# Column tiles for the 384-column products of the second pass, in a four-layer graph kernel

## The chip, the cores and the metric

The kernel runs on one core of one Trainium2 chip. The metric is the device time of one execution in microseconds (us); less is better. The core's engines each work through their own instruction stream in order: TensorE (PE, with its weight loads shown apart as PEld), VectorE (DVE), ScalarE (ACT), GpSimd (POOL) and SyncE (SP), which here issues most of the DMA transfers. Engines wait for each other by semaphores.

## The reference, cut to what matters

There are 32 graphs (batches) of 512 nodes with 128 features, each with a symmetric 0/1 adjacency matrix. Four layers follow one another, and each adds its result to `x`:

```python
h = relu(layernorm(x))                       # before each layer
# layer 0: masked attention
q, k, v = relu(h @ Wq.T + bq), relu(h @ Wk.T + bk), relu(h @ Wv.T + bv)
x = x + softmax(mask(q @ k.T, adj)) @ v
# layer 1: convolution of the last 128 nodes -> LSTM over 128 steps -> gates a normalized aggregation
dyn = conv(h[:, -128:, :]); lw = lstm(dyn)
x = x + sigmoid((A_norm @ h) @ lw)
# layer 2: four graph layers with skip connections; layer 3: one aggregation, a product and a PReLU
x = x + layer2(h, adj);  x = x + prelu(adj @ (h @ W.T) + bias)
```

What matters for the order of the work is layer 1. Its LSTM needs layer 0's result for the last 128 nodes of all 32 batches, and then runs 128 steps one after another. The layers from 1 on need its end.

## The kernel before

The kernel is one program of some 26,400 instructions. The function `symmetric` builds a list of operations, and a planner (`class Plan`) puts them in order with assumed durations. The order that it finds is each engine's fixed instruction stream; on the chip nothing is reordered by it any more.

**The stages.**

- *Pass 1* (`pass_1(b)`, ranks from 10,000): for each batch, `x` is loaded and normalized, keys and values are computed, layer 0 is finished for the last 128 nodes alone, and the convolution fills the LSTM's input `seq`. Keys, normalized input and values go to DRAM.
- *The LSTM* (`lstm()`, ranks 0 to 127, all below `URGENT`): 128 steps. A step's products have a 128-row by 32-column weight tile (the hidden state of 32 batches), so four of them, each for another 32 features, stand side by side in the array and run together. This is what the code calls tiled (`tiled=True`). Each step has 16 matrix instructions of this kind (`f_z`, L1212), since an fp32 product is two instructions.
- *Pass 2* (`pass_2(b)`, ranks from 20,000): layer 0 for the other 384 nodes of each batch. It is independent of the LSTM and is meant to fill the engines beside it. Per batch it has one query product `f_pq` (L1291) and four score products `f_s` (L1300), each 128 by 128 by 384 columns, then an exponential (L1303), a product with the mask (L1304), twelve products `f_po` (L1309) and an update of `x`. For batches in `EARLY` (0 to 19) layer 1's aggregation `f_pg` (L1395) is done here too.
- *The rest* (`rest(b, turn, lw_after)`, ranks from 30,000): layers 1 to 3 of each batch, after the LSTM.

**What sets the order.** An operation's rank is its priority. The planner takes for each engine the operation that can start earliest, and among those that can start at once the lowest rank. A rank of 30,000 or more is replaced by a due time. `LATE = 4` gives the pass 2 of the last four batches such a rank, so that they are due among the first turns of the rest; `FIRST` names the two batches before them, whose rest comes first. Two costs are written into the planner for a change between tiled and other products on TensorE, of which this is the first and this the place that makes it count in the choice:

```python
    SWITCH = (0.2, 0.1)          # to a product that is not tiled, to one that is
    ...
                    if e == "PE" and o.tiled != tiled and rank >= self.spared:
                        s = max(s, free[e] + self.SWITCH[o.tiled])
```

`self.spared` is 20,000. So after a tiled operation a tiled one that is ready starts 0.2 sooner than one that is not tiled, whatever the ranks; after one that is not tiled, it is the tiled one that comes 0.1 later. The LSTM's steps are kept from delay by `held`: an operation of rank 1000 or more is not started where it would run more than 0.15 us beyond the expected start of a step.

**Buffers.** `BUFS` gives the number of each tag; the tags `ar`, `x`, `inv`, `n0` to `n3` and `a` are handed out in the order in which the program names them. PSUM has eight banks (`mm`).

**Transfers and warming.** `DMA` books a transfer on SP and adds `gap=2.0` us until its data counts as landed. `warm_up` books products on a tile of zeros, whose results nobody reads, in front of the first real products: 16 at the start, and 16 more in the last turn.

Of the kernel before, what the change touches and what calls it, by code (L numbers as in the profile page):

```python
# [13 lines left out]
P = 128  # L14
# [6 lines left out]
W_Q, W_K, W_V, W_CONV, W_IH, W_HH = 0, 1, 2, 3, 6, 10  # L21
# [731 lines left out]
def symmetric(ctx, tc, x, adj, weights, cols, rows, lstm_b, prelu_a, out, fail):  # L753
# [12 lines left out]
    nc = tc.nc  # L766
# [3 lines left out]
    L = NT - 1  # L770
    NR = N - P
    MANY = 512 // (4 * B)
    LATE = 4
    FIRST = [B - LATE - 2 + k for k in range(2)]
    EARLY = range(20)
    FOLDS = (4, 7, 10, 13)
    MOVED = range(2, B - 2)
    TURN = 32
# [3 lines left out]
    BUFS = {"a": 2, "ar": 6, "x": 7, "xn": 5, "y": 5, "gs": 5, "inv": 4, "n0": 4, "n1": 4, "n2": 4, "n3": 4, "low": 3, "hp": 2, "dt": 2, "mm": 8, "st": 4, "mv": 4, "rs": 4, "sh": 4, "dg": 8, "dv": 4,  # L782
            "ri": 3, "th": 3, "c": 3, "cu": 2, "cv": 2, "tcn": 2, "h": 2}
# [10 lines left out]
    plan = Plan(BUFS, ("ar", "x", "inv", "n0", "n1", "n2", "n3", "a"), "mm")  # L794
# [4 lines left out]
    def f32(ap):  # L799
        return ap.bitcast(FP)  # L800
# [5 lines left out]
    def new(tag, shape, name, dtype=FP):  # L806
        return plan.cell(sb, tag, shape, dtype, name)

    def bank(name, shape=(P, 512), whole=True, filled=False):
        return plan.cell(ps, "mm", shape, FP, name, whole, filled)  # L810


    def t_mm(n):
        return max(0.222, n * 0.001676)
# [6 lines left out]
    def t_act(n):  # L821
        return 0.17 + n * 0.0006

    def t_dve(n):
        return 0.145 + n * 0.00088

    def t_dma(kb):
        return 0.1 + kb / 315.0

    def PE(rank, t, fn, r=(), w=(), **k):  # L830
        return plan.op({"PE": (t, fn)}, rank, r, w, **k)

    def ACT(rank, t, fn, r=(), w=(), **k):
        return plan.op({"ACT": (t, fn)}, rank, r, w, **k)

    def DVE(rank, t, fn, r=(), w=(), **k):
        return plan.op({"DVE": (t, fn)}, rank, r, w, **k)

    def POOL(rank, t, fn, r=(), w=(), **k):
        return plan.op({"POOL": (t, fn)}, rank, r, w, **k)  # L840

    def DMA(rank, kb, fn, r=(), w=(), **k):
        return plan.op({"SP": (max(0.45, t_dma(kb)), fn)}, rank, r, w, gap=2.0, **k)

    def turn_tiles(dst, src):

# [37 lines left out]
    w = const.tile([P, W_SD[0] + 1, P], FP, name="f_w")  # L884
# [27 lines left out]
    for j in range(P // TURN):  # L912
        part = bass.ts(j, TURN)
# [8 lines left out]
    def warm_up(rank, t, name, after=()):  # L922

        c = bank(name)
        PE(rank, t, lambda: nc.tensor.matmul(c.t, marks[:, :P], marks, start=True, stop=True), [], [c], after=after)

    for k in range(2 * BUFS["mm"]):
        warm_up(HEAD, 0.43 if k < 8 else 0.216, f"f_warm_{k}")

    def bias_row(rank, k, row, r):  # L930
# [174 lines left out]
    def pass_1(b):  # L1105
        R = 10_000 + b * 10
        xc = new("x", (P, NT, P), f"f_x_{b}")
        DMA(R, 256, lambda: nc.sync.dma_start(xc.t, x[b].rearrange("(t p) d -> p t d", p=P)), [], [xc])
        al = new("n1", (P, NT, P), f"f_al_{b}")
        DMA(R + 11, 256, lambda: nc.sync.dma_start(al.t, adj[b, :, NR:].rearrange("(t p) i -> p t i", p=P)), [], [al])  # L1110
        xn = ln_full(R, xc, f"a{b}")
# [36 lines left out]
        s = bank(f"f_sl_{b}", (P, NT, P))  # L1148
# [117 lines left out]
    def pass_2(b):  # L1266
        R = 20_000 + b * 10 if b < B - LATE else 30_000 + (b - B + LATE) * 10 + 15
        dkq, dv, dl, dx = kept[b]
        early = b in EARLY
        whole = early or b in FIRST  # L1270
        a = new("a" if whole else "ar", (P, NT, N if whole else NR), f"f_a_{b}")
        keys = new("inv", (P, N), f"f_k2_{b}")
        hT = new("xn", (P, NR), f"f_h2_{b}")
        v = new("n3", (P, NT, P + 1), f"f_v2_{b}")
        xc = new("x", (P, NT if whole else L, P), f"f_x2_{b}")
        DMA(R, 192, lambda: nc.sync.dma_start(hT.t, dkq.t[:, N:]), [dkq], [hT])
        DMA(R, 256, lambda: nc.sync.dma_start(keys.t, dkq.t[:, :N]), [dkq], [keys])
        if whole:
            DMA(R, 1024, lambda: nc.sync.dma_start(a.t, adj[b].rearrange("(t p) j -> p t j", p=P)), [], [a])
            ar, deg = squares(R, b, a, "2")  # L1280
            mask, rows_of = ar, lambda j: f32(ar.t[:, j, :NR])
        else:
            DMA(R, 768, lambda: nc.sync.dma_start(a.t, adj[b, :, :NR].rearrange("(t p) j -> p t j", p=P)), [], [a])
            mask, rows_of = a, lambda j: a.t[:, j, :]
        DMA(R, 258, lambda: nc.sync.dma_start(v.t, dv.t), [dv], [v])
        DMA(R, 192, lambda: nc.sync.dma_start(xc.t[:, :L, :], x[b, :NR].rearrange("(t p) d -> p t d", p=P)), [],
            [(xc, t) for t in range(L)])
        if whole:
            DMA(R, 64, lambda: nc.sync.dma_start(xc.t[:, L, :], dl.t), [dl], [(xc, L)])
        pq = bank(f"f_pq_{b}", (P, NR), whole=False)  # L1290
        PE(R, t_mm(NR), lambda: nc.tensor.matmul(pq.t, w[:, W_Q, :], hT.t, start=True, stop=True), [hT], [pq])  # L1291
        q = new("xn", (P, NR), f"f_q_{b}")
        plan.op({
            "ACT": (t_act(NR) + 0.09, lambda: nc.scalar.activation(q.t, pq.t, AF.Relu, bias=colb[:, C_Q : C_Q + 1])),
            "DVE": (t_dve(NR), lambda: nc.vector.tensor_scalar(q.t, pq.t, colb[:, C_Q : C_Q + 1], 0.0, OP.add, OP.max)),
        }, R, [pq], [q])
        es = []
        for j in range(NT):
            s = bank(f"f_s_{b}_{j}", (P, NR), whole=False)
            PE(R, t_mm(NR), lambda s=s, j=j: nc.tensor.matmul(s.t, keys.t[:, bass.ts(j, P)], q.t, start=True, stop=True),  # L1300
               [keys, q], [s])
            e = new(f"n{j}" if j < 3 else "y", (P, NR), f"f_e_{b}_{j}")
            ACT(R, t_act(NR), lambda s=s, e=e: nc.scalar.activation(e.t, s.t, AF.Exp), [s], [e])  # L1303
            DVE(R, t_dve(NR), lambda e=e, j=j: nc.vector.tensor_mul(e.t, e.t, rows_of(j)), [(mask, j)], [e])  # L1304
            es.append(e)
        po = bank(f"f_po_{b}", (P, L, P + 1), whole=False)
        for t in range(L):
            for j in range(NT):
                PE(R, t_mm(P), lambda t=t, j=j: nc.tensor.matmul(  # L1309
                    po.t[:, t, :], es[j].t[:, bass.ts(t, P)], v.t[:, j, :], start=(j == 0), stop=(j == NT - 1)),  # L1310
                    [es[j], v], [po])
        ri = plan.fixed(None)
        sum_ops.append(DVE(R, 0.21, lambda: nc.vector.reciprocal(rinv[:, b, :L], po.t[:, :, P]), [po], [ri]))
        for t in range(L):
            DVE(R, 0.26, lambda t=t: nc.vector.scalar_tensor_tensor(xc.t[:, t, :], po.t[:, t, :P], rinv[:, b, t : t + 1],
                                                                    xc.t[:, t, :], OP.mult, OP.add), [po, ri], [(xc, t)])
        if whole and not early:
            begun[b] = a, xc, ar, deg
        else:
            DMA(R + 5, 192, lambda: nc.sync.dma_start(dx.t, xc.t[:, :L, :]), [(xc, t) for t in range(L)], [dx])  # L1320
        mv = ln_stats(R, xc, range(L), f"r{b}")
        l1 = lns[b]
        POOL(R, 0.15, lambda: nc.gpsimd.tensor_copy(ln1[:, b, 0, :L], mv.t[:, :L, 0]), [mv], [(l1, "mr")])
        ln_rstd(R, mv, 0, L, (lambda: ln1[:, b, 1, :L], (l1, "rr")))
        if early:
            d = new("dg", (P, NT), f"f_d2_{b}")

            def root():
                nc.gpsimd.tensor_scalar_add(d.t, deg.t, 1.0)
                nc.gpsimd.tensor_tensor(d.t, d.t, neg_half[:, 0, :], OP.pow)  # L1330
            POOL(R, 1.3, root, [deg], [d])
            rs = new("rs", (P, NT), f"f_rs_2{b}")
            POOL(R, 0.34, lambda: nc.gpsimd.tensor_mul(rs.t, ln1[:, b, 1, :], d.t), [d, l1], [rs])
            gT, _ = sums_of_1(R, b, xc, ar, rs)
            dg = plan.fixed(dram.tile([P, N], FP, tag=f"g{b}", name=f"f_dgT_{b}"))
            DMA(R + 5, 256, lambda: nc.sync.dma_start(dg.t, flat(gT.t)), [gT], [dg])
            kept_sums[b] = dg
# [5 lines left out]
    def squares(rank, b, a, name):  # L1343

        ar = new("ar", (P, NT, N), f"f_ar{name}_{b}", FR)
        deg = new("dg", (P, NT), f"f_deg{name}_{b}")
        for t in range(NT):
            ACT(rank, 0.62, lambda t=t: nc.scalar.activation(ar.t[:, t, :], a.t[:, t, :], AF.Square,  # L1348
                                                             accum_out=deg.t[:, t : t + 1]), [a], [(ar, t), (deg, t)])
        return ar, deg  # L1350
# [226 lines left out]
    for b in range(B):  # L1577
        pass_1(b)
# [94 lines left out]
```

## Time and profile before

| | before |
|---|---|
| time, median of 3 runs | 1316.56 us (1314.63 to 1316.73) |
| span of the profiled run | 1316.2 us |
| busy: PE, PEld | 1288.5, 990.8 us |
| busy: DVE, ACT, POOL | 999.4, 826.0, 392.7 us |
| granted TensorE clock, mean | 0.995 |
| LSTM steps on TensorE | 188.4 to about 506 us |

A line of the profile's groups reads: line of the code, engine, operation, output tile and input tiles, shapes, count, then busy time and mean nanoseconds of one, then the idle time of the engine ahead of them and what ended it. Matrix products are pipelined: the duration of one includes its way through the array, so two that follow each other overlap, and the distance between their starts is what each costs. A line of the timeline reads: start, length, engine, line, operation, output and inputs, count merged into the line.

### The profile page before, as it was taken

What the parts mean: (1) busy time and instruction counts of PE and PEld (TensorE: products, weight loads), DVE (VectorE), ACT (ScalarE), POOL (GpSimd) and SP (SyncE); (2) the same over time, 40 slices, a digit from 0 to 9 for tenths busy, and PEclk for the clock granted to TensorE, in tenths of its full rate; (3) what the DMA queues carried; (4) which work ended last, traced back from release to release, by engine and by line L of the source; (5) the groups of instructions that cost most, each with busy time, mean ns of one, the idle gap of its engine ahead of it and who ended that gap; (6) DMA issues with size and microseconds to landing.
All of it is one profiled execution on the core that took longest, in us unless ns stands there. A gap on an engine that the chain in (4) does not pass through costs nothing. (4 is left out here: it accounts for less than half of the span.)

```text
span 1316.2 us, 26405 instructions
## 1 busy us (share of the span) xinstructions
PE 1288.5 (98%) x8829; PEld 990.8 (75%) x8829; DVE 999.4 (76%) x3392; ACT 826.0 (63%) x2084; POOL 392.7 (30%) x729
## 2 busy tenths in 40 slices
PE   8999999999999999999999999999999999999996
PEld 6888876776766766777777787787877877877774
DVE  7888878887788788766588668777777887787744
ACT  5666667777765655676387547576665675675433
POOL 4655533321221133331142224132232332332101
PEclk8999999999999999999999999999999999999999
DMA  7888888887676656975568766767645566673211
GB/s 230 266 262 271 261 282 288 265 278 238 204 245 199 194 176 108 229 191 139 105 135 218 166 153 128 193 151 152 156 120 120 121 136 140 142 168 64 54 28 36
DMA packets 298817, 230.69 MB, mean 175 GB/s; under 512 B 138032, under 2 KB 245808, under 8 KB 298672
## 3 DMA queue, kind: packets, MB, share of 16 engines
q1 hardware_dynamic: 281776, 212.13, 57.4%
q0 software_dynamic: 16896, 16.78, 8.3%
q8 instruction: 72, 1.18, 0.4%
q14 instruction: 73, 0.60, 0.2%
HBM read 135.80 MB, written 61.60 MB: 150 GB/s over the span
## 5 line engine op out<-in xcount | busy, mean ns | idle before, releaser
L1395 PE MATMUL f_pa<-f_ar,f_y 128*128 128x512 f32 x1024 | 292.8, 422 | 0.7 <-ACT f_y L1377 0.7
L1395 PEld LDWEIGHTS f_pa<-f_ar,f_y 128*128 128x128 f32 x1024 | 188.2, 188 | 66.2 <-issue 28.0
L1489 PE MATMUL f_py<-f_wf,f_n 128*128 128x128 f32 x1280 | 173.9, 275 | 0.2 <-ACT f_n L1504 0.2
L1489 PEld LDWEIGHTS f_py<-f_wf,f_n 128*128 128x128 f32 x1280 | 163.8, 192 | 9.2 <-ACT f_n L1504 1.9
L1504 ACT ACTIVATE f_n<-f_pa,f_bcol 128x512 f32<-128x512 f32 x128 | 88.0, 689 | 110.5 <-PE f_pa L1500 107.2
L1500 PE MATMUL f_pa<-f_n,f_wf 128*128 128x512 f32 x320 | 152.7, 593 | 1.1 <-DVE f_pa L1496 1.1
L1348 ACT ACTIVATE f_ar<-f_a 128x512 fp32r<-128x512 f32 x208 | 129.1, 622 | 13.4 <-DMA f_a<-in_adj_dram 6.7
L1377 ACT CAST f_y<-f_py 128x512 fp32r<-128x512 f32 x128 | 74.6, 583 | 87.0 <-PE f_py L1489 81.5
L1309 PEld LDWEIGHTS f_po<-f_v,f_e 128*128 128x128 f32 x768 | 100.7, 190 | 25.5 <-issue 10.9
L1496 DVE TENSOR_TENSOR f_pa<-f_pa,f_inv 128x512 f32<-128x512 f32 x128 | 87.5, 693 | 41.0 <-PE f_pa L1395 40.5
L1378 DVE TENSOR_TENSOR f_y<-f_py,f_y 128x512 fp32r<-128x512 f32 x128 | 87.3, 684 | 34.5 <-ACT f_y L1377 34.4
L1309 PE MATMUL f_po<-f_v,f_e 128*128 128x129 f32 x768 | 112.7, 282 | 0.6 <-DVE f_e L1304 0.6
L1300 PE MATMUL f_s<-f_q,f_k 128*128 128x384 f32 x256 | 99.7, 500 | 0.0
L1457 POOL DMA_DIRECT2D f_das<-f_ar x32 | 28.8, 899 | 230.9 <-ACT f_ar L1348 126.4
L1500 PEld LDWEIGHTS f_pa<-f_n,f_wf 128*128 128x128 f32 x320 | 56.8, 190 | 44.5 <-issue 37.0
L1462 DVE SCALAR_TENSOR_TENSOR f_junk<-f_a,f_aT 128x1024 bf16<-128x1024 f32 x64 | 78.1, 1221 | 7.6 <-DMA f_aT<-f_das 6.5
L1212 PE MATMUL f_z<-f_w,f_seq 128*32 128x128 f32 x2040 | 82.2, 279 | 1.6 <-DVE f_seq L1260 0.6
L1395 PE MATMUL f_pg<-f_ar,f_xp_d 128*128 128x512 f32 x256 | 77.9, 428 | 0.0
L1212 PEld LDWEIGHTS f_z<-f_w,f_seq 128*32 128x32 f32 x2040 | 48.3, 109 | 37.4 <-ACT f_e L1303 7.2
L1395 PE MATMUL f_pg<-f_ar,f_xp_c 128*128 128x512 f32 x256 | 72.4, 412 | 0.3 <-ACT f_xp_c L1385 0.3
L1489 PE MATMUL f_py<-f_wf,f_T_c 128*128 128x128 f32 x448 | 72.7, 275 | 0.0
L1303 ACT ACTIVATE f_e<-f_s 128x384 f32<-128x384 f32 x128 | 61.2, 487 | 16.1 <-PE f_s L1300 14.5
(203 smaller groups left out, 2738.7 us busy)
## 6 DMA issues: line engine op xcount, KB each, us to landing
f_a<-in_adj_dram SPq DMA_DIRECT2D x52, 1024.0 KB
f_das<-f_ar POOLq DMA_DIRECT2D x32, 512.0 KB, 5.3
f_dkq<-f_kh SPq DMA_DIRECT2D x32, 448.0 KB
f_dv<-f_v SPq DMA_DIRECT2D x32, 258.0 KB
f_v<-f_dv SPq DMA_DIRECT2D x32, 258.0 KB
f_x<-in_x_dram SPq DMA_DIRECT2D x32, 256.0 KB
f_al<-in_adj_dram SPq DMA_DIRECT2D x32, 256.0 KB
f_k<-f_dkq SPq DMA_DIRECT2D x32, 256.0 KB
```

Of the source, the lines that this page charges most:

```text
L1212: nc.tensor.matmul(z.t[part, k, :, :], h, w[:, m : m + 4, part], start=False, stop=True, skip_group_check=True)
L1300: PE(R, t_mm(NR), lambda s=s, j=j: nc.tensor.matmul(s.t, keys.t[:, bass.ts(j, P)], q.t, start=True, stop=True), [keys, q], [s])
L1309: PE(R, t_mm(P), lambda t=t, j=j: nc.tensor.matmul(po.t[:, t, :], es[j].t[:, bass.ts(t, P)], v.t[:, j, :], start=(j == 0), stop=(j == NT - ...
L1348: ACT(rank, 0.62, lambda t=t: nc.scalar.activation(ar.t[:, t, :], a.t[:, t, :], AF.Square, accum_out=deg.t[:, t : t + 1]), [a], [(ar, t), ...
L1377: ACT(rank, t_act(N), lambda: nc.scalar.copy(parts.t[:, :, 0, :], src.t), [src], [(parts, 0)])
L1378: DVE(rank, t_dve(N), lambda: nc.vector.tensor_sub(parts.t[:, :, 1, :], src.t, f32(parts.t[:, :, 0, :])), [src, (parts, 0)], [(parts, 1)])
L1395: nc.tensor.matmul(pg.t, parts.t[:, j, k, :], ar.t[:, j, :], start=(k == 0 and j == 0), stop=(k == 1 and j == NT - 1))
L1462: nc.vector.scalar_tensor_tensor(junk, flat(a.t[:, 2 * k : 2 * k + 2, :]), 1.0, flat(aT.t[:, 2 * k : 2 * k + 2, :]), OP.mult, OP.not_equal ...
L1489: nc.tensor.matmul(py.t[:, j, :], nodes[n].t[:, bass.ts(j, P)], wf[:, W_F[i] + c, 0, :], start=False, stop=(c == nch - 1), skip_group_chec ...
L1496: before = DVE(R, t_dve(N), lambda pa=pa: nc.vector.tensor_mul(pa.t, pa.t, inv_row.t), [inv_row], [pa])
L1500: nc.tensor.matmul(pa.t, wf[:, W_F[i] + c, 1, :], nodes[n].t, start=False, stop=(c == nch - 1), skip_group_check=True)
L1504: ACT(R, 0.57, lambda pa=pa, n=n, i=i: nc.scalar.activation(n.t, pa.t, AF.Tanh, bias=bcol[:, i : i + 1]), [pa], [n])
```

## The change

Four edits are made.

- The query and score products of pass 2 are written as four products of 32 columns of the stationary matrix each, one per column tile of the array (`by_columns`), and are booked with `tiled=True`. The result in PSUM is the same. The aim is that they stand beside the LSTM's tiled products without a change of the array's mode.
- `LATE` becomes 5: the pass 2 of one more batch (27) is due among the first turns of the rest, and `FIRST` becomes batches 25 and 26.
- The planner's landing time of the loads of `x` in pass 1 is 2.0 us for batch 0, 4.5 us for batches 1 to 3 and 3.5 us for the others, where it was 2.0 us for all.
- The products that warm TensorE at the start become 20, where they were 16 (`2 * BUFS["mm"]`).

```diff
-    LATE = 4
+    LATE = 5
     FIRST = [B - LATE - 2 + k for k in range(2)]
...
     def DMA(rank, kb, fn, r=(), w=(), **k):
-        return plan.op({"SP": (max(0.45, t_dma(kb)), fn)}, rank, r, w, gap=2.0, **k)
+        return plan.op({"SP": (max(0.45, t_dma(kb)), fn)}, rank, r, w, gap=k.pop("gap", 2.0), **k)
+
+    def by_columns(out, left, right):
+        for c in range(P // TURN):
+            part = bass.ts(c, TURN)
+            nc.tensor.matmul(out[part], left[:, part], right, start=True, stop=True)
...
-    for k in range(2 * BUFS["mm"]):
+    for k in range(20):
         warm_up(HEAD, 0.43 if k < 8 else 0.216, f"f_warm_{k}")
...
-        DMA(R, 256, lambda: nc.sync.dma_start(xc.t, x[b].rearrange("(t p) d -> p t d", p=P)), [], [xc])
+        DMA(R, 256, lambda: nc.sync.dma_start(xc.t, x[b].rearrange("(t p) d -> p t d", p=P)), [], [xc],
+            gap=2.0 if b == 0 else 4.5 if b < 4 else 3.5)
...
-        PE(R, t_mm(NR), lambda: nc.tensor.matmul(pq.t, w[:, W_Q, :], hT.t, start=True, stop=True), [hT], [pq])
+        PE(R, t_mm(NR), lambda: by_columns(pq.t, w[:, W_Q, :], hT.t), [hT], [pq], tiled=True)
...
-            PE(R, t_mm(NR), lambda s=s, j=j: nc.tensor.matmul(s.t, keys.t[:, bass.ts(j, P)], q.t, start=True, stop=True),
-               [keys, q], [s])
+            PE(R, t_mm(NR), lambda s=s, j=j: by_columns(s.t, keys.t[:, bass.ts(j, P)], q.t),
+               [keys, q], [s], tiled=True)
```

## The prediction

> **What bounds the kernel now.** I read the page's first part, then the busy times by stage, then the timeline of TensorE inside the LSTM's stage, and last the head of the run. The page says that TensorE is the engine to look at.
>
> ```profile
> PE 1288.5 (98%) x8829; PEld 990.8 (75%) x8829; DVE 999.4 (76%) x3392; ACT 826.0 (63%) x2084; POOL 392.7 (30%) x729
> ```
>
> The stages, cut at the LSTM's first step, its last, and the last product of pass 2:
>
> ```profile
> core 0: us, PE busy (x) PEld busy (x) DVE busy (x) ACT busy (x) POOL busy (x), PEclk, DMA share, GB/s
> 0.00:188.00 188.00, 179.83 (x1278) 152.95 (x1279) 154.59 (x687) 115.63 (x227) 96.57 (x247) 0.98 0.83 262
> 188.00:507.00 319.00, 315.68 (x3260) 219.94 (x3259) 257.85 (x1179) 223.18 (x781) 80.77 (x152) 1.00 0.72 226
> 507.00:545.00 38.00, 35.06 (x223) 28.86 (x222) 30.70 (x107) 22.64 (x59) 14.32 (x25) 1.00 0.89 183
> 545.00:1316.00 771.00, 757.94 (x4072) 589.05 (x4070) 556.27 (x1423) 464.58 (x1018) 201.08 (x307) 1.00 0.59 133
> ```
>
> TensorE is full everywhere, so only what shortens its stream, or fills its holes, can count. Busy time hides the holes that matter, because the tail of one product covers them. So I went through the start times in the timeline and took from each distance between two starts the usual distance for the product (0.111 us for 128 columns fp32, 0.323 for 384, 0.429 for 512, 0.231 for 512 in the reduced format). What remains is lost time: 18.3 us in pass 1, 45.0 in the LSTM's stage, 3.7 up to 545 us and 7.0 in the rest. Of the 45.0, this is the larger part:
>
> ```profile
> 302.80 0.27 PE L1309 MATMUL f_po<-f_v,f_e 128*128 128x129 f32 x1
> 303.00 0.32 PE L1212 MATMUL f_z<-f_w,f_seq 128*32 128x128 f32 x4
> 303.13 0.51 PE L1212 MATMUL f_z<-f_w,f_seq 128*32 128x128 f32 x12
> 303.57 0.73 PE L1395 MATMUL f_pg<-f_ar,f_xp_c 128*128 128x512 f32 x2
> ```
>
> One step of the LSTM: four rounds of four tiled instructions. The way in: 0.20 us after the last `f_po` instead of 0.11, and the first round takes 0.13 instead of 0.11, together 0.11. The way out: the fourth round starts at 303.35 and should be through at 303.46; `f_pg` starts at 303.57, 0.11 later, and two of them take 0.73 us where the second, some 0.40 long, should start 0.23 after the first: 0.10 more, since the first weight load stands open. A visit to the tiled mode costs 0.11 + 0.11 + 0.10 = 0.32 us, by the mean of all 128 visits 0.116 + 0.119 + 0.10 = 0.335. 128 visits make 43 us.
>
> What stands between two steps decides whether a visit can be saved:
>
> ```profile
> 325.46 0.65 PE L1212 MATMUL f_z<-f_w,f_seq 128*32 128x128 f32 x16
> 326.04 1.56 PE L1300 MATMUL f_s<-f_q,f_k 128*128 128x384 f32 x4
> 327.72 0.65 PE L1212 MATMUL f_z<-f_w,f_seq 128*32 128x128 f32 x16
> 328.29 0.91 PE L1300 MATMUL f_s<-f_q,f_k 128*128 128x384 f32 x2
> 329.04 0.39 PE L1309 MATMUL f_po<-f_v,f_e 128*128 128x129 f32 x2
> 329.26 0.81 PE L1300 MATMUL f_s<-f_q,f_k 128*128 128x384 f32 x2
> 329.91 0.39 PE L1309 MATMUL f_po<-f_v,f_e 128*128 128x129 f32 x2
> 330.23 0.64 PE L1212 MATMUL f_z<-f_w,f_seq 128*32 128x128 f32 x16
> ```
>
> Steps follow each other every 2.50 us on average (318/127), at the shortest 2.14. Of the 127 stretches between steps I count 11 with nothing but `f_pq` and `f_s` (as at 326.04), 68 mixed, 48 with neither.
>
> The head of the run, by the windows in which the clock is granted:
>
> ```profile
> 6.33:9.74 3.41, 1.55 (x9) 0.73 (x7) 1.69 (x9) 0.49 (x1) 0.00 (x0) 1.00 1.08 313
> 9.74:13.15 3.41, 2.72 (x6) 1.43 (x7) 2.79 (x16) 1.43 (x3) 1.27 (x2) 0.50 1.11 287
> 13.15:16.57 3.42, 3.42 (x18) 3.42 (x17) 2.83 (x16) 1.54 (x3) 2.28 (x4) 0.50 0.61 212
> 1303.40:1306.80 3.40, 2.15 (x13) 1.38 (x11) 1.65 (x3) 1.00 (x2) 0.00 (x0) 1.00 0.26 77
> ```
>
> After a window with 1.55 us of PE the clock is halved for two windows; after one with 2.15 us, near the end, it stays. And the loads of `x` in pass 1, by what waits for them:
>
> ```profile
> 8.05 0.49 DVE L1027 BATCH_NORM_STATS2 f_st_a<-f_x 128x6 f32<-128x128 f32 x2 [3.28 <-DMA f_x<-in_x_dram]
> 8.63 0.49 ACT L1047 ACTIVATE f_xn_a<-f_x,f_sh_a,f_rs_a 128x128 f32<-128x128 f32 x1 [6.40 <-DVE f_sh_a L1055]
> DVE f_st_a L1027 <- DMA f_x<-in_x_dram: 10.3, 8, 3.3
> ```
>
> VectorE stands 3.28 us at batch 1's `x`, with batch 0's normalization queued behind it, though that one's scale was ready on GpSimd at 6.2. In all 10.3 us in 8 waits.
>
> **What the Trainium skill says.** "TensorEngine Tiling (Array Packing)", section Tiling Modes, says that a change of tiling mode drains the engine, and that tiles load weights and multiply independently. The trace agrees: 0.335 us per visit, and four `f_z` start within 0.02 us and share one 0.11 us round. "TensorE: Matmul & The Clock Gate", Part 1, says that the clock falls to half after a window of about 3.4 us in which the engine is idle; here one that is 45% busy was enough (1.55 of 3.41).
>
> **The change part by part.**
>
> *Tiled products, the stream itself.* A 384-column product is two instructions 0.323 us apart, 0.65 us in all. In column tiles it is eight, in two rounds of four. If four run together as `f_z` does, a round streams the same 384 columns in 0.323 us: 0.65 again, plus 0.02 of stagger. The trace has no tiled product of this width. Its bounds are 0.65 and, if the four did not overlap at all, 4 x 0.65 = 2.6; `f_z` reads four streams at full rate, so I take 0.65. ACT's exponential waits for the last tile: 0.02 later, hidden by PE's backlog. Where a weight load stands open, 32 columns cost 0.02 and 128 cost 0.10; worth a few tenths in all.
>
> *Tiled products, the visits.* Putting a tiled product behind a step saves nothing alone: the way out is paid later, behind the product. A visit is saved only if two steps have nothing but tiled products between them. The planner now prefers ready tiled products right behind a step, whatever their rank, so in the mixed stretches `f_s` comes first and in one piece, and three of them (3 x 0.65 = 1.94 us) just fit between two steps. Before, 11 stretches were pure; with one such group in most of some 26 batches I take 27. Three-product stretches save 0.335 each, two-product ones less, as the chain of the LSTM itself then sets the 2.14 us; two thirds of 27 x 0.335 = 6.0. I book 5 us. Ends: 2 (no new pure stretch) and 12 (40 stretches at nearly full value).
>
> *Tiled products outside the LSTM.* Before 188 us and after the LSTM each group of tiled products is a visit of its own, at 0.335 us. 12 `f_s` start after 507 us now, three batches; with one more late batch some four, with two groups each (query, then scores): 8 x 0.335 = 2.7 us. In pass 1, 8 `f_s` and 3 `f_pq`, some 3 visits, 1.0 us, half of it in holes. The planner also puts tiled products behind any other ready product there. Queued behind them are the first turns of the rest, because `inv`, `x` and `n0` to `n3` are handed out in program order. I book +3; ends +1 and +8.
>
> *LATE = 5.* It moves batch 27's 5 x 0.65 + 24 x 0.111 = 5.9 us of PE from a stage where PE is full to one where it is full too: 0, with -2 and +2 as ends.
>
> *Landing times.* They change no transfer, only what is put ahead of the waiting instruction. The waits on `x` after 16 us are 10.3 - 2.3 - 3.3 = 4.7 us on DVE, and holes of 0.53, 0.66, 0.63, 0.95 and 0.33 us on PE lie at five of them (98, 114, 117, 145 and 164 us): 3.1 us. I take 2 of it. At the head, batch 0's normalization no longer stands behind batch 1's load: its transposes can start near 8.0 (the end of the warming products) instead of 9.2: 1.1 us.
>
> *Warming.* Four products more, 4 x 0.216 = 0.86 us, in a hole of 2.0 us: hidden. They bring the window from 6.33 to 9.74 to 1.55 + 0.86 = 2.4 us busy, above the 2.15 that kept the clock. The half clock cost (2.72 + 3.42)/2 = 3.1 us of PE work; DVE is 2.8 of 3.4 us busy there and will hold some of it back: I take 2. Pass 1 in all: 2 + 1 + 2 = 5 us; ends 1 and 7.
>
> Sum: -5 (pass 1) -5 (visits) +3 (visits elsewhere) +0 = -7, from 1316.6 to 1309.6; with a few tenths from open weight loads, 1309.
>
> **The rivals.**
>
> *Visits outside eat the gain.* For it: a stretch with two scores and two `f_po` costs the same in either order, and most mixed stretches are such. Then visits save 2, elsewhere cost 5, pass 1 gives 3: 1316.6, no change. Against it: 27 batches bring four scores each that become ready together.
>
> *Slower: tiled products are starved.* They wait for a hole in other work wherever there is no LSTM step, and the rest's buffers wait for them. A stall at the border of, say, 6 us (PE lost 3.7 there before), +8 for visits, -2 visits saved, -5 in pass 1 and -0: 1323 or so. If the four tiles did not overlap, 160 products x up to 1.9 us more would make far over 1400, which I give next to nothing. For it: the freshly laid order can be worse anywhere. Against it: holes in the rest are only 7.0 us of 771, and the planner books the changes of mode at 0.3.
>
> *More than forecast.* Nearly every batch gives a pure stretch or two (-12), pass 1 gives 7, elsewhere +2: 1299. Against it: the LSTM's own chain, some 2.1 us a step.
>
> **How the numbers follow.** Forecast 0.55, no change 0.18, starved 0.14, more 0.13. A neighbourhood of 4 us of the forecast stays below 1314, so faster by over 0.2% (under 1313.9) takes it nearly whole, the last rival, and a little of the second: 0.74; same 0.13; slower 0.13. The range from 1299 to 1319 takes in the last rival and leaves out most of the starved case.
>
> **What would show it.** Each step of the 128 still a visit except in pure stretches; 20 to 40 of these. `f_s` as eight instructions in two rounds 0.32 us apart. The clock at 1.00 from 6.33 on, DVE's waits for `x` below 4 us, and the LSTM's first step near 183 us instead of 188.4. Steps every 2.40 us or less. `f_s` in the rest in groups, PE's lost time there under 15 us. It is wrong if rounds of tiled products are longer than 0.33 us, if pure stretches stay near 11, or if PE stands idle where the LSTM ends.

## The result, and the profile after

The changed kernel took 1332.70 us (median of four runs, 1328.51 to 1339.63); the kernel before took 1316.64 us beside it (four runs, 1314.63 to 1318.56). The ratio is 1.0127, with a 95% interval of 1.0078 to 1.0176: slower, outside the predicted range of 1299 to 1319. The profiled execution of the changed kernel, with a span of 1326.6 us, is the fastest of its four, so the trace shows 10.4 us of the difference and not all 16.

The first part of the page after, and the granted clock along the span in 40 slices:

```profile
PE 1281.9 (97%) x9798; PEld 979.2 (74%) x9798; DVE 1003.5 (76%) x3395; ACT 824.8 (62%) x2081; POOL 381.1 (29%) x729
PEclk9999999998999999999999999999999999999998
```

TensorE is busy 6.6 us less than before (1288.5), in a span that is 10.4 us longer. So the stream did get shorter, and holes came in. The windows by stage, cut at the same events as before:

```profile
core 0: us, PE busy (x) PEld busy (x) DVE busy (x) ACT busy (x) POOL busy (x), PEclk, DMA share, GB/s
0.00:180.00 180.00, 176.21 (x1332) 147.72 (x1332) 153.41 (x684) 113.75 (x227) 91.43 (x245) 1.00 0.87 275
180.00:516.00 336.00, 313.33 (x4174) 210.98 (x4174) 257.23 (x1167) 226.39 (x793) 75.64 (x150) 0.98 0.67 212
516.00:547.50 31.50, 31.22 (x231) 27.35 (x220) 24.88 (x90) 17.45 (x43) 12.61 (x22) 1.00 0.82 185
547.50:1326.60 779.10, 761.15 (x4080) 593.11 (x4078) 567.94 (x1456) 467.25 (x1018) 201.40 (x314) 0.99 0.60 134
```

The LSTM's first step starts at 180.1 us (188.4 before): 8.3 us gained. From the first step to the last it takes 335.7 us (317.7 before): 18.0 us lost, and in that stage TensorE is idle for 336.0 - 313.3 = 22.7 us, where it was 3.3. From the last step to the end it is 810.8 us (810.1): 0.7 lost. Together +10.4. The DMA share of the LSTM's stage (the mean busy share of the core's 16 DMA engines) has *fallen*, from 0.72 to 0.67: whatever the engines wait for there, the transfer engines are not full on average.

By the distances of the 128 steps' starts, three were over 2.9 us before, and together exceeded the usual 2.5 us by 2.9 us. After, 12 are, by 21.9 us. The others average 2.467 us, against 2.477. The loss lies in a few stalls; one is 6.8 us long. The timeline of the changed kernel there (start, length, engine, line, operation, and in brackets the idle time ahead and what ended it):

```profile
406.79 0.62 PE L1221 MATMUL f_z<-f_w,f_seq 128*32 128x128 f32 x16
...
412.32 0.60 DVE L1052 TENSOR_SCALAR f_x<-f_x,f_ln,f_rs 128x128 f32<-128x128 f32 x2 [3.23 <-DMA f_dx<-f_x]
412.38 0.49 ACT L1055 ACTIVATE f_x<-f_x,f_sh_c,f_rs 128x128 f32<-128x128 f32 x1 [3.38 <-DMA f_dx<-f_x]
412.78 0.21 ACT L1264 ACTIVATE f_tcn<-f_c 128x32 f32<-128x32 f32 x1
...
413.61 0.65 PE L1221 MATMUL f_z<-f_w,f_seq 128*32 128x128 f32 x16 [4.03 <-DVE f_seq L1269]
```

Read it from the bottom. The step waits for `f_seq`, which comes from `f_tcn` on ScalarE. `f_tcn`'s input was ready at 409.1. But ScalarE works in order, and ahead of `f_tcn` stands the normalization of another batch, in place in its `x` buffer. It may overwrite `x` only when `x` has been stored (`f_dx`), and it waits 3.4 us for that store. So a transfer that nobody needs soon holds the LSTM. Why is it late? SyncE's timeline of the same stretch:

```profile
396.79 0.32 SPq L1345 DMA_DIRECT2D f_dgT<-f_x  x1
399.61 0.32 SPq L1294 DMA_DIRECT2D f_v<-f_dv  x1
403.30 0.38 SPq L1295 DMA_DIRECT2D f_x<-in_x_dram  x1
403.74 0.48 SPq L1288 DMA_DIRECT2D f_a<-in_adj_dram  x1
404.31 0.46 SPq L1329 DMA_DIRECT2D f_dx<-f_x  x1
```

The `x` to be stored was complete on VectorE at 401.3. SyncE issues its store only at 404.31, because it issues in order too and stands at L1295, a load of another batch's `x` into a buffer that is itself still being stored (`f_dgT`, issued at 396.79). When that store is through, the load goes out, then a load of 1 MB (`f_a`), and only then the `f_dx` store. The store lets the engines go at 412.3, 8.0 us after its issue. The plan books 0.71 + 2.0 us for it.

SyncE's own waits in the LSTM's stage (us in total, times, longest), first before, then after:

```profile
SPq L1286 <- DMA f_dgT<-f_x: 26.1, 9, 5.9
...
SPq L1286 <- DMA f_dx<-f_x: 9.8, 5, 2.7
```

```profile
SPq L1295 <- DMA f_dgT<-f_x: 52.0, 17, 6.6
...
SPq L1295 <- DMA f_dx<-f_x: 22.6, 5, 6.1
```

It is the same line of the code. SyncE stood there for 35.9 us before and 74.6 after. What the engines wait for from transfers in the same stage, after:

```profile
DVE f_x L1052 <- DMA f_dx<-f_x: 9.6, 5, 3.2
```

```profile
PE f_pc L1023 <- DMA f_w<-in_weights_dram: 5.3, 1, 5.3
```

ScalarE has 8.6 us of such waits. In all that is 24.2 us after (9.6 on VectorE, 8.6 on ScalarE, 6.0 on TensorE), against 3.0 before. They overlap in part, so their sum is a sign and not the price.

The wait of 5.3 us belongs to the largest stall, a step that takes 8.2 us from 296.7 on. It too begins with SyncE: the weights `f_w` were issued at 297.98, after a load of `x` at which SyncE had stood for 6.6 us:

```profile
286.94 1.16 SPq L1345 DMA_DIRECT2D f_dgT<-f_x  x1
294.73 0.38 SPq L1295 DMA_DIRECT2D f_x<-in_x_dram  x1
...
297.98 0.36 SPq L985 DMA_DIRECT2D f_w<-in_weights_dram  x1
```

The place in the planner is the line that says when a buffer is free again: `c.free_at = max(c.free_at, o.end)`. For a store, `o.end` is the end of its issue; the 2.0 us to its landing count for those who read the stored data, not for the buffer. So the planner may put the reload of an `x` buffer straight behind the store that empties it, and on the chip SyncE stands there until the store is through. `x` has seven buffers.

### The profile page after: what moved, and what is told of

It is laid out like the page before. It is cut to its first block, busy times and chain, and to the rows that moved or that the text cites. A ratio compares the mean times of both kernels' runs of the same rounds, so it can differ in the third digit from the quotient of the medians.

```text
span 1326.6 us, 28360 instructions
## 1 busy us (share of the span) xinstructions
PE 1281.9 (97%) x9798; PEld 979.2 (74%) x9798; DVE 1003.5 (76%) x3395; ACT 824.8 (62%) x2081; POOL 381.1 (29%) x729
## 5 line engine op out<-in xcount | busy, mean ns | idle before, releaser
L1498 PEld LDWEIGHTS f_py<-f_wf,f_n 128*128 128x128 f32 x1280 | 165.0, 192 | 10.3 <-ACT f_n L1513 1.8
L1318 PEld LDWEIGHTS f_po<-f_v,f_e 128*128 128x128 f32 x768 | 96.5, 192 | 23.1 <-issue 17.4
L1318 PE MATMUL f_po<-f_v,f_e 128*128 128x129 f32 x768 | 107.5, 282 | 0.1
L851 PE MATMUL f_s<-f_q,f_k 128*32 128x384 f32 x1024 | 95.2, 487 | 1.3 <-DMA f_k<-f_dkq 0.7
L1221 PEld LDWEIGHTS f_z<-f_w,f_seq 128*32 128x32 f32 x2040 | 51.6, 110 | 44.9 <-ACT f_e L1312 9.0
L1055 ACT ACTIVATE f_xn_c<-f_x,f_sh_c,f_rs_c 128x128 f32<-128x128 f32 x138 | 58.3, 487 | 20.8 <-DVE f_sh_c L1063 20.7
```

The costliest lines, as they stand in the source:

```text
L851: nc.tensor.matmul(out[part], left[:, part], right, start=True, stop=True)
L1221: nc.tensor.matmul(z.t[part, k, :, :], h, w[:, m : m + 4, part], start=False, stop=True, skip_group_check=True)
L1318: PE(R, t_mm(P), lambda t=t, j=j: nc.tensor.matmul(po.t[:, t, :], es[j].t[:, bass.ts(t, P)], v.t[:, j, :], start=(j == 0), stop=(j == NT - ...
L1498: nc.tensor.matmul(py.t[:, j, :], nodes[n].t[:, bass.ts(j, P)], wf[:, W_F[i] + c, 0, :], start=False, stop=(c == nch - 1), skip_group_chec ...
```

## The experiments

They are in four groups. Each ran beside the kernel before on the same chip (1318.1 to 1318.5 us there); ratios are to that, with 95% intervals. "Waits on transfers" are those of VectorE, ScalarE and TensorE in the LSTM's stage of the profiled execution; "SyncE's waits" are those for stores at L1295 in the same stage. The expectations use these names. A: the stalls were hidden before because the engines trailed the plan, and the corrected pass 1 takes that slack away. B: they come from the order that the tiled products bring. C: they come from the late batch. P: tiled instructions themselves disturb the others. D: SyncE stands at the reload of an `x` buffer whose store isn't through. E: only the planned landing time of the `f_dx` store is short. V: the visits saved by tiles are worth several us once transfers do not stall.

### Which part of the change

`e1_tiles` has the tiled products alone:

```diff
-    LATE = 5
+    LATE = 4
-    for k in range(20):
+    for k in range(2 * BUFS["mm"]):
-            gap=2.0 if b == 0 else 4.5 if b < 4 else 3.5)
+            gap=2.0)
```

> Only the column tiles; LATE, landing times and warming products as before. Theory A (the planner's 2.0 us for every transfer beside the LSTM is too short, and before the change this was hidden because the engines ran some 10 us behind the plan when the LSTM began): the LSTM begins near 188 us as before, waits on transfers of DVE, ACT and PE beside it stay under 6 us (2.9 before, 24 after), its stage takes some 310 us, total 1308 to 1314. Theory B (the order that the tiles bring puts dependents too close behind their transfers): waits of 15 us or more, stage 325 us or more, total 1325 to 1340.

It took 1337.58 us (1329.45 to 1341.15), ratio 1.0126 [1.0076, 1.0177], with 65.8 us of SyncE's waits, 17.4 us of waits on transfers and an LSTM stage of 329.2 us. That is what B expected: the tiles alone bring the loss. But the stage is only part of it here. In the profiled execution (1339.4 us) it is 11.5 us longer than before, and the part after the LSTM's last step is 16.5 us longer (826.6, where it was 810.1). No run shows why.

`e4_tiles_late` adds the late batch, with pass 1 as before:

```diff
-    for k in range(20):
+    for k in range(2 * BUFS["mm"]):
-            gap=2.0 if b == 0 else 4.5 if b < 4 else 3.5)
+            gap=2.0)
```

> Tiles and LATE = 5, pass 1 as before. Theory A: LSTM from 188 us, waits on transfers under 6 us, total 1308 to 1314. Theory B: as the changed kernel with the 8 us of pass 1 given back, 1335 or more.

1345.52 us (1343.83 to 1349.40), 1.0213 [1.0172, 1.0254]; SyncE's waits 77.5 us, waits on transfers 31.0, stage 333.5, the part after it 827.5. It stalls as much without the corrected pass 1, so A is not needed for the loss, with one reserve: in both kernels the LSTM begins at 183 us and not at 188, as fewer tiled products are taken into pass 1 (four `f_s` and two `f_pq`, where they were eight and three).

`e2_pass1` has only the landing times and the 20 warming products:

```diff
-    LATE = 5
+    LATE = 4
-        PE(R, t_mm(NR), lambda: by_columns(pq.t, w[:, W_Q, :], hT.t), [hT], [pq], tiled=True)
+        PE(R, t_mm(NR), lambda: nc.tensor.matmul(pq.t, w[:, W_Q, :], hT.t, start=True, stop=True), [hT], [pq])
```

and the scores likewise.

> Only the landing times of pass 1 and the 20 warming products; no tiles, LATE = 4. Theory A: the LSTM begins near 180 us, and its stage then shows waits on transfers of 10 us or more, stage 328 us or more, total 1314 to 1325. Theory B: the 8 us of pass 1 stay, stage 318 us, total 1307 to 1311.

1314.05 us (1309.22 to 1322.90), 0.9965 [0.9948, 0.9981]. The LSTM begins at 183.9 us: 4.5 gained, while the kernel gains 4. The median is near what B expected (1307 to 1311) and at the lower end of A's range. The profiled execution, of 1321.0 us, is the slowest of 18, and it is as A expected: 47.6 us of SyncE's waits, 16.4 us of waits on transfers and a stage of 327.5 us, without a single tiled score. So such stalls can also come without any tiles, with the order that the edits of pass 1 bring. With a spread of 14 us this run decides less than the other three.

`e5_no_late` is the changed kernel with `LATE = 4`:

```diff
-    LATE = 5
+    LATE = 4
```

> The changed kernel with LATE = 4. If the late batch is the cause (theory C), the waits on transfers beside the LSTM fall under 6 us and the total to 1303 to 1310; by theories A and B they stay at 15 us or more and the total at 1322 to 1340.

1335.57 us (1334.38 to 1340.53), 1.0143 [1.0102, 1.0185]; SyncE's waits 80.0 us, waits on transfers 20.4. The stalls stay without the late batch, so C falls.

### The tiles, or the order they bring

`e6_order_only` keeps the changed kernel's order (`tiled=True` for the planner) and gives TensorE the full 128-column products:

```diff
-        PE(R, t_mm(NR), lambda: by_columns(pq.t, w[:, W_Q, :], hT.t), [hT], [pq], tiled=True)
+        PE(R, t_mm(NR), lambda: nc.tensor.matmul(pq.t, w[:, W_Q, :], hT.t, start=True, stop=True), [hT], [pq], tiled=True)
```

> The changed kernel's order on every engine, instruction for instruction, but with each 384-column product written as one product of 128 stationary columns. If the tiled instructions themselves disturb something (theory P), waits on transfers of DVE, ACT and PE beside the LSTM fall below 8 us and the total, with some 35 visits paid again at 0.335 us, is 1318 to 1326. If the order does it (theory B), those waits stay at 12 us or more and the total is 1330 to 1348.

1345.76 us (1342.54 to 1351.39), 1.0227 [1.0192, 1.0262]; SyncE's waits 70.0 us, waits on transfers 15.9. The loss stays when not one of these products is tiled, so P falls and B holds: it is the order. Its steps without a stall average 2.560 us, against 2.467 in the changed kernel: in this order the tiles save some 0.09 us on each of 116 such steps, about 11 us of visits. The kernel is 13 us slower than the changed one, but that isn't the price of these visits. In the profiled executions the LSTM's stage is only 3.9 us longer (339.6), since its stalls are smaller, and the part after it is 11.0 us longer (821.8), where one score product is left; why is not shown.

`e7_slots` makes the planner keep a buffer until its store has landed, and books 5.0 us for the `f_dgT` store:

```diff
-                c.free_at = max(c.free_at, o.end)
+                c.free_at = max(c.free_at, o.end + (o.gap if o.engine == "SP" else 0.0))
...
-            DMA(R + 5, 256, lambda: nc.sync.dma_start(dg.t, flat(gT.t)), [gT], [dg])
+            DMA(R + 5, 256, lambda: nc.sync.dma_start(dg.t, flat(gT.t)), [gT], [dg], gap=5.0)
```

> The changed kernel, with the planner holding a buffer that a transfer reads or writes until the transfer's gap is over (before, until it was issued), and a gap of 5 us for the store of the layer-1 sums. Theory D (SyncE stands at the reload of an x buffer whose store is not through, so that all transfers behind it come late and in a burst): SyncE's waits for that store fall from 52 us to under 25, waits on transfers of DVE, ACT and PE from 24 us to under 10, total 1308 to 1318. Theory E (only the landing time of the store of x, 2.0 us in the plan, matters): waits of DVE and ACT for that store stay at 12 us or more, total 1324 to 1340.

1312.15 us (1311.19 to 1312.70), 0.9951 [0.9924, 0.9978]: 20 us faster than the changed kernel, and faster than before. SyncE's waits in its LSTM stage:

```profile
SPq L1295 <- DMA f_dgT<-f_x: 8.8, 5, 3.0
...
SPq L1295 <- DMA f_dx<-f_x: 8.3, 5, 2.3
```

17.1 us where there were 74.6, the waits on transfers are 5.9 us where there were 24.2, and the stage is 319.0 us. VectorE and ScalarE wait 3.5 us for the `f_dx` store, where E expected 12 or more. This speaks for D. But the edit also lays a new order everywhere, so it isn't proof yet.

### How much of it, and what the tiles are worth then

`e8_slots_landings` books 4.0 us for every transfer that has no time of its own; `e9_store4` leaves the buffers alone and corrects only the `f_dx` store; `e10_fixed_no_tiles` has the planner mended and no tiles:

```diff
 e8
-                c.free_at = max(c.free_at, o.end)
+                c.free_at = max(c.free_at, o.end + (o.gap if o.engine == "SP" else 0.0))
-        return plan.op({"SP": (max(0.45, t_dma(kb)), fn)}, rank, r, w, gap=k.pop("gap", 2.0), **k)
+        return plan.op({"SP": (max(0.45, t_dma(kb)), fn)}, rank, r, w, gap=k.pop("gap", 4.0), **k)
```

```diff
 e9
-            DMA(R + 5, 192, lambda: nc.sync.dma_start(dx.t, xc.t[:, :L, :]), [(xc, t) for t in range(L)], [dx])
+            DMA(R + 5, 192, lambda: nc.sync.dma_start(dx.t, xc.t[:, :L, :]), [(xc, t) for t in range(L)], [dx], gap=4.0)
```

```diff
 e10: as e8, with 5.0 in place of 4.0, and
-        PE(R, t_mm(NR), lambda: by_columns(pq.t, w[:, W_Q, :], hT.t), [hT], [pq], tiled=True)
+        PE(R, t_mm(NR), lambda: nc.tensor.matmul(pq.t, w[:, W_Q, :], hT.t, start=True, stop=True), [hT], [pq])
```

> As e7_slots, but with 4.0 us for every transfer instead of 5 us for the one store. Theories D and E both have their cause taken away: waits of DVE, ACT and PE on transfers beside the LSTM under 6 us, total 1300 to 1312. If neither is the cause, 1322 or more.

1307.76 us (1305.85 to 1310.67), 0.9927 [0.9903, 0.9950]. SyncE's wait at the reload and the window of the LSTM's stage:

```profile
SPq L1295 <- DMA f_dgT<-f_x: 1.1, 2, 0.8
```

```profile
182.60:497.50 314.90, 307.69 (x4134) 205.84 (x4130) 250.86 (x1150) 224.33 (x792) 72.87 (x141) 0.99 0.71 223
```

VectorE, ScalarE and TensorE's products wait for no transfer in this stage now. It takes 314.9 us, shorter than before (317.7), and TensorE is idle 7.2 us of it, not 22.7.

> The changed kernel with a planned gap of 4.0 us for the store of x alone. Theory E: waits of DVE and ACT for that store fall from 16 us to under 6, total 1308 to 1318. Theory D: SyncE's waits stay at 50 us or more, the other waits only move to other transfers, total 1320 to 1340.

1325.65 us (1318.72 to 1330.10), 1.0073 [1.0046, 1.0100]: some 7 us of the loss come back. SyncE still stands there:

```profile
SPq L1295 <- DMA f_dgT<-f_x: 55.1, 18, 5.5
```

With its waits for the `f_dx` store that is 60.8 us. Neither theory is met in full. The total is in D's range and not in E's. But the waits on transfers fall from 24.2 to 6.8 us (2.9 of them for the `f_dx` store), where D expected them to move to other transfers. And in the profiled execution, the fastest of its runs (span 1316.8 us), the LSTM's stage takes 316.5 us, no more than before (317.7), with SyncE standing as long as ever. The part after the LSTM is longer there (818.9 us, where it was 810.8 in the changed kernel), for a reason that no run shows. So a stand on SyncE doesn't cost time by itself. It costs where an engine's next instruction is placed close behind a transfer that the stand makes late, and the planned landing time decides how close. This edit lays a new order, so that reading is argued.

> As e8_slots_landings, but without column tiles and with 5.0 us for every transfer (at 4.0 us the planner's order without tiles has holes of its own). If the tiles' saved visits are worth what was forecast once the transfers no longer stall (theory V), this is 4 to 9 us slower than e8: 1311 to 1318. If the tiles are worth nothing, it is within 3 us of e8: 1305 to 1311.

1314.01 us (1313.34 to 1316.26), 0.9971 [0.9961, 0.9981], stage 315.6 us, no wait for transfers. It is 1314.0 - 1307.8 = 6.2 us slower than `e8_slots_landings`, as V expected. Between the two lie the tiles, the order that they bring and 1.0 us of booked landing time. In the profiled executions 2.3 us of the difference lie before the LSTM, 0.8 in its stage and 2.3 behind it. That saved visits make up the 6.2 us is not shown.

### The same order without the stand

The edits to the plan move every instruction. `e11_x8` keeps the changed kernel's order of instructions exactly: the planner still counts seven `x` buffers, but there are eight in memory, so each reload goes into one whose store is a turn older. To make room, a comparison of the adjacency with its transpose writes its unread elementwise result over its own input and not into a scrap tile:

```diff
-            return pool.tile(shape, dtype, tag=tag, name=name, bufs=BUFS[tag])
+            return pool.tile(shape, dtype, tag=tag, name=name, bufs=BUFS[tag] + (tag == "x"))
...
-                nc.vector.scalar_tensor_tensor(junk, flat(a.t[:, 2 * k : 2 * k + 2, :]), 1.0, flat(aT.t[:, 2 * k : 2 * k + 2, :]),
+                nc.vector.scalar_tensor_tensor(flat(aT.t[:, 2 * k : 2 * k + 2, :]), flat(a.t[:, 2 * k : 2 * k + 2, :]), 1.0, flat(aT.t[:, 2 * k : 2 * k + 2, :]),
```

> The changed kernel's order on every engine, but with eight x buffers in memory where the planner still counts seven, so that a reload of an x buffer no longer stands at the store of the batch before (the room comes from writing the result of the symmetry comparison, which nobody reads, over its own input). Theory D: SyncE's waits for the stores of x and of the sums fall from 75 us to under 15, waits of DVE, ACT and PE on transfers from 24 us to under 10, total 1308 to 1319. If SyncE's standing is a companion and not the cause: total 1324 to 1340.

1310.86 us (1306.17 to 1311.57), 0.9929 [0.9903, 0.9956]: 21.8 us faster than the changed kernel with the same order. SyncE's waits for stores at L1295:

```profile
SPq L1295 <- DMA f_dx<-f_x: 0.4, 1, 0.4
```

The waits for `f_dgT` there are gone. At the place of the stall shown first, `f_dgT`, `f_v`, `f_x`, `f_a` and `f_dx` now go out at 388.29, 391.11, 391.48, 391.96 and 392.86: SyncE issues the load of `x` 0.37 us after that of `v`, where it took 3.69. The largest stall is gone too: the load of `x` now leaves 0.37 us after the store, `f_w` at 291.79, and TensorE finds the weights there:

```profile
287.29 0.32 SPq L1345 DMA_DIRECT2D f_dgT<-f_x  x1
287.66 0.43 SPq L1295 DMA_DIRECT2D f_x<-in_x_dram  x1
...
291.79 0.33 SPq L985 DMA_DIRECT2D f_w<-in_weights_dram  x1
```

```profile
299.27 0.28 PE L1023 MATMUL f_pc<-f_colb,f_w 128*128 128x1 f32 x2
```

In the changed kernel that line reads:

```profile
304.39 0.34 PE L1023 MATMUL f_pc<-f_colb,f_w 128*128 128x1 f32 x1 [5.32 <-DMA f_w<-in_weights_dram]
```

In the profiled executions the LSTM's stage is 321.9 us (335.7), and the part after it 807.4 (810.8). So some 14 of the 18.0 us that the stage had lost come back. VectorE and ScalarE still wait 9.7 us for `f_dx` stores, and the transfer waits in all are 12.4 us, more than the 10 expected: that is E's part, the landing time, which eight buffers don't change. The store issued at 392.86 lets its waiters go at 400.65, still 7.8 us later. But it leaves as soon as its data is complete on VectorE (392.83), and not 3.0 us after that.

`e12_best_x8` puts eight buffers and `e8_slots_landings` together:

```diff
 e8, and
-            return pool.tile(shape, dtype, tag=tag, name=name, bufs=BUFS[tag])
+            return pool.tile(shape, dtype, tag=tag, name=name, bufs=BUFS[tag] + (tag == "x"))
```

with the comparison's result placed as in `e11_x8`.

> e8_slots_landings with eight x buffers in memory. Its SyncE waits at x buffers are 1 us already, so by theory D nothing is left to gain there: within 2 us of e8, 1305 to 1310.

1307.22 us (1306.66 to 1309.26), 0.9913 [0.9886, 0.9940]: no measurable difference from `e8_slots_landings`, as there is nothing left to remove. This run also tests the other half of `e11_x8`'s edit: the moved comparison result is in it too, and the part after the LSTM is 809.0 us, against 809.1. Where nothing stands at the stores, that half is worth nothing that can be seen. Both kernels beat the one before by some 0.8%.

## Why the prediction was wrong

**The step that failed** is its first, "TensorE is full everywhere, so only what shortens its stream, or fills its holes, can count". It read how full TensorE was in the old order and took it for a property of the stage, so it has no place for what opens new holes. The change lays a new order for every engine, SyncE's too, and the sum puts the effect of that on the transfers at nothing (for the landing times, "They change no transfer"). The second rival says that "the freshly laid order can be worse anywhere", but gives it no size and no mechanism. SyncE's waits of the kernel before, which the prediction did not read, already showed 35.9 us at the reload of `x`. The missing term is the 18.0 us by which the LSTM's stage grew: TensorE's holes in it went from 3.3 to 22.7 us. `e11_x8` shows the cause of most of it: with the same order and one more buffer the kernel takes 21.8 us less, and the stage some 14. What is left of the 18.0 stands beside 12.4 us of waits on transfers, whose landing times that run leaves as they are.

**Pass 1, -5:** the LSTM begins 8.3 us earlier. The two edits of pass 1 have 4.5 us of it alone (`e2_pass1`) and 2.6 when added to the tiles (182.7 in `e4_tiles_late`, 180.1 after). Tiled products that are no longer taken into pass 1 give some of the rest, but in the changed kernel only two are missing there (one `f_s`, one `f_pq`), 1.3 us by 0.65 each; what the others owe is not shown. The steps held: VectorE's waits for `x` fell from 10.3 us to

```profile
DVE f_st_a L1035 <- DMA f_x<-in_x_dram: 2.4, 1, 2.4
```

and the clock at the head stays full:

```profile
5.18:8.59 3.41, 2.88 (x16) 1.38 (x13) 2.30 (x10) 0.98 (x2) 1.04 (x1) 1.00 0.96 287
8.59:12.00 3.41, 3.25 (x21) 2.60 (x21) 2.17 (x14) 1.77 (x5) 1.27 (x2) 1.00 1.19 295
12.00:15.40 3.40, 2.57 (x14) 1.50 (x13) 3.20 (x16) 1.99 (x5) 1.58 (x2) 1.00 1.11 355
```

**The stream of tiled products, 0.65 us as before:** right. Pure stretches now look so:

```profile
309.27 0.61 PE L1221 MATMUL f_z<-f_w,f_seq 128*32 128x128 f32 x16
309.71 2.11 PE L851 MATMUL f_s<-f_q,f_k 128*32 128x384 f32 x24
311.65 0.61 PE L1221 MATMUL f_z<-f_w,f_seq 128*32 128x128 f32 x16
```

Three products in 1.94 us between the starts, 0.65 each, with nothing paid for the way in or out. Their rounds start 0.32 us apart.

**The visits, -5, from 27 pure stretches:** there are 35 (11 before), so the premise held and more. What they are worth is known only roughly: about 11 us of shorter steps by `e6_order_only` in the changed kernel's order, and 6.2 us in the whole time from `e10_fixed_no_tiles` to `e8_slots_landings`, with another order. The mean unstalled step is 2.467 us, where 2.40 was forecast.

**The visits outside, +3:** the part after the LSTM took 0.7 us more. That is nearer to the forecast's lower end (+1) than to +3, and for another reason. The premise was wrong twice. The `f_s` that start after the last step were nine products before and not twelve, and they became one, not more: the tiled ones are drawn forward into the LSTM's stage.

**`LATE = 5`, nothing:** with the corrected pass 1, 1335.6 without it and 1332.7 with it; the ranges overlap. With pass 1 as before it is not nothing: `e4_tiles_late` is 8 us slower than `e1_tiles`, and their ranges don't overlap. Each edit lays another order, so its effect depends on the others. In the changed kernel it did not even move the work out: 120 `f_s` start between the first and the last step, 111 before.

**The rivals.** The starved case came nearest in time (1323), but by another way. It put the stall where the LSTM ends and most of the loss, 8 us, on visits. In the changed kernel TensorE is idle for only 0.3 us from the last step to the end of pass 2, and 3.2 us in one piece behind that, at 553.5. That is like before (2.9 us up to 545).

**What stays open.** Why the kernel before bore 35.9 us of SyncE's waits with only 3.0 us of transfer waits on the other engines is not tested; its reloads stood nine times at the `f_dgT` store, those after 17 times, and `e9_store4` has a stage without loss with 60.8 us of them. `LATE = 5` without tiles in the planner as it was wasn't tried. The part after the LSTM, alike in the kernel before and the changed one, is 9 to 17 us longer in `e1_tiles`, `e4_tiles_late`, `e6_order_only` and `e9_store4`, and 3.4 us shorter in `e11_x8`; neither is explained. So a few us between two kernels with different orders can't be put down to one part of an edit.

## What to carry to other kernels

When a change makes a planner lay a new order, read the queues of every engine that issues in order, the transfers' own included, before calling any of them idle: a wait on SyncE holds up all the transfers behind it, and appears on other engines as a late transfer where they need one soon. In a static plan a buffer that is stored is free when the store has landed, not when it is issued. To tell the order from the wait in it, keep the order and give one more buffer, as `e11_x8` does.

## What the runs showed of the hardware

A store of 192 KB issued right behind loads of 192 KB and 1 MB released its waiters 8.0 us after its issue (404.31 to 412.32), and 7.8 us after it in `e11_x8` (392.86 to 400.65).

Four column tiles of 384 columns keep the rounds of 128-column ones in proportion: 0.32 us for the round, 0.65 us for an fp32 product, as for the untiled one.

A stall costs more than its length. TensorE waits for the weights from 299.07 to 304.39 us in the changed kernel; the windows around it, laid where the granted clock changes:

```profile
298.70:302.10 3.40, 0.37 (x4) 0.18 (x2) 1.11 (x5) 0.35 (x1) 2.47 (x5) 1.00 0.76 165
302.10:305.50 3.40, 1.11 (x14) 1.09 (x18) 0.00 (x0) 0.00 (x0) 0.00 (x0) 0.51 1.01 355
305.50:308.90 3.40, 3.40 (x32) 1.18 (x24) 1.78 (x8) 1.47 (x5) 0.00 (x0) 0.50 1.05 404
308.90:312.30 3.40, 3.40 (x65) 1.73 (x58) 2.70 (x10) 2.56 (x10) 0.00 (x0) 0.99 0.96 322
```

When the weights are there, TensorE comes back to a clock of half the speed and works through the window from 305.5 to 308.9 us with it, full all the time. After the stall shown first the same follows:

```profile
411.40:414.80 3.40, 1.19 (x19) 0.93 (x20) 2.31 (x9) 1.95 (x6) 0.00 (x0) 1.00 0.61 221
...
414.80:418.20 3.40, 3.40 (x27) 2.80 (x25) 1.01 (x4) 0.40 (x3) 0.00 (x0) 0.50 0.21 80
```

The clock is halved at four places of this kernel between 302 and 702 us, for 6.8 us and three times 3.4 us. In `e11_x8`, with the same order, it isn't halved in the LSTM's stage at all. By an estimate from the windows above, 7.9 us of TensorE's work in that stage (1.11 + 3.40 + 3.40) ran at half the speed, which is some 4 us on top of the stalls. "TensorE: Matmul & The Clock Gate", Part 1, of the Trainium skill says that an idle window halves the clock; here windows with 0.37, 1.11 and 1.19 us of work in 3.4 were followed by the half clock, while at the head one with 2.57 us was not. Between these the busy time alone doesn't decide: 1.63 us (407.95 to 411.36) left the clock full, and 1.78 us in `e8_slots_landings` (277.25 to 280.67) were followed by the half clock.
